# Two-bank PSUM tiles written whole before they are read, and other work moved between them, in a graph network layer

## The chip, the cores and the metric

The kernel runs on one core of a Trainium2 chip. The metric is device time in microseconds (us) of one execution. The engines of the core work side by side, each through its own list of instructions in order: TensorE (PE) multiplies matrices, VectorE (DVE) and ScalarE (ACT) work on elements, GpSimd (POOL) and SyncE (SP) here mostly start DMA transfers. An instruction waits until those whose results or buffers it needs are done. PSUM is the small memory that TensorE writes its results into; the kernel uses it in banks of 128 partitions by 512 fp32 numbers, two for each of its tiles.

## What is computed

One layer over 64 graphs of 256 nodes with 256 features (fp32). Cut to what matters:

```python
h = relu(layernorm(x))                                  # [64, 256, 256]
xc = h.transpose(0, 2, 1)
c = relu(bn1(conv1d(xc, conv1_w, pad=0)))               # 1 tap: 256 x 256 product
c = bn2(conv1d(c, conv2_w, pad=8))                      # 17 taps
x_conv = relu(c + xc).transpose(0, 2, 1)
s = h @ w_se.T + b_se                                   # 3 numbers for each node
dist = sq[:, :, None] + sq[:, None, :] - 2 * s @ s.T    # sq = sum(s * s)
A = exp(-dist) * adj
msg = relu(h @ w_msg.T + b_msg)
x_nmp = A @ msg
gi = concat(x_conv, x_nmp) @ w_ih.T + b_ih              # 3 gates of 256
gh = h @ w_hh.T + b_hh
r, z = sigmoid(gi_r + gh_r), sigmoid(gi_z + gh_z)
n = tanh(gi_n + r * gh_n)
out = x + (1 - z) * n + z * h
```

## The kernel before

The 64 graphs are worked on in pairs, numbered i = 0 to 31; a tile of one pair holds 2 x 256 = 512 nodes in its columns and 128 features in its partitions. Four pairs make a block, and there are eight blocks (b = 0 to 7; i = 4b is the block's first pair and nxt = i + 4 the next block's first). The trace's fifth block works on pairs 16 to 19.

**The convolution of 17 taps** is done for a block at once, by a transform along the nodes: conv1(j) (lines 673 to 688) makes each pair's input h, `split_steps` and `forward` (odd and even steps, which end with the tiles Sv, and U and PT) transform it on DVE (lines 59 to 65, with some scales on ACT, line 68), `begin(m)` and `complete(m)` (m = 0 to 7) multiply the bins by filters that SP streams from DRAM into nine buffers named wb, and the inverse (branch_back, odd_back, q_back, p_back, and a join for each pair) brings it back into Yv. `residual` (lines 817, 818) adds h and applies the relu for a pair. While a block's products run, the inputs of the block behind it are normalised (norm_steps), turned into feature-by-node layout by DMA (turn_h, sort_h, join_h; the result is hT) and run through conv1.

**Messages:** `message(i)` multiplies hT by w_msg and w_se on PE, adds the bias on DVE (line 830) and makes z, four small ACT operations, and the relu; `embed(i)` transposes z on PE and copies it into zT on ACT; `affinity(i)` multiplies zT with itself on PE, takes exp on ACT and multiplies by adj on DVE (line 868); `aggregate(i)` makes xnm from e and msg.

**Gates:** `gates(i)` (lines 1006 to 1074) forms the r and z gates as a block product with seven parts instead of eight, from hT, xnm and Yv (named "h", "xn", "xc") and sums of their quarters that DVE makes (sums_a line 937, sums_b line 945), in buffers wb that the filters give up for a while. `ghn(i)` (lines 995 to 1002) is the n gate's product of h, Gn that of the other inputs; DVE joins them (lines 1052, 1061), ACT takes tanh, DVE makes the output tr (lines 1069 to 1074), and `finish(i)` transposes it back, adds x and stores it (lines 1076 to 1091). Only the first pair of a block passes late_xc: its part 1 begins with h and xn, and the xc terms come once the inverse has got as far as this pair.

**What sets the order.** The order of each engine's list is that of the Python program, written by hand; gates takes functions (after5, fill, after7, after4, after) that it calls between its parts, and other work is put there. Only the DVE steps of the transforms float: they stand in a queue, `pace.vector` lets out as many as fit before the next DVE operation by a small model of PE's and DVE's time, and `pace.flush` lets out all up to a mark.

**PSUM.** All PE results go through two names, aux and acc, each with two buffers, and each buffer is a tile of two banks ([128, 2, 512] fp32). The third tile of a name waits until the readers of the first are done. All matmuls stand in the trace under the line of a helper, 516 (transposes 520), so a row is known by its output and inputs.

Of the kernel before, what the change touches and what calls it, by code (L numbers as in the profile page):

```python
# [300 lines left out]
def kernel(  # L301
# [372 lines left out]
    def conv1(i, bank=aux):  # L674
        if i >= B // G:
            return
        p = bank()
        for o in range(DC):
            for k in range(DC):
                mm(p[:, o], w_c1[:, k, o * P:(o + 1) * P], HT[i][:, k, :], W, start=(k == 0), stop=(k == DC - 1))  # L680
            v = h1.rearrange("p (g o) s b -> p o g s b", o=DC)[:, o, :, :, 1:1 + NW]
            u = p[:, o].rearrange("p (g s b) -> p g s b", g=G, b=NW)
            if i == 0:
                nc.vector.tensor_scalar(v, u, s1[:, o:o + 1], h1_shift[:, o:o + 1], ALU.mult, ALU.add)
                nc.vector.tensor_scalar(v, v, 0.0, None, ALU.max)
# [135 lines left out]
    def message(i):  # L821
        MSG[i] = work.tile([P, G, MC, D + SE], FP, name="msg")
        for g in range(G):
            p = aux()
            for c in range(MC):
                for k in range(DC):
                    mm(p[:, c, :D + SE], chunk(HT[i][:, k], g, c), w_msg[:, k, :], D + SE,
                       start=(k == 0), stop=(k == DC - 1))
            pace.vector(MC * D, pace.pe + PSUM)
            nc.vector.tensor_add(MSG[i][:, g], p[:, :, :D + SE], b_msg.unsqueeze(1).to_broadcast([P, MC, D + SE]))  # L830
        s = MSG[i][:, :, :, D:]
        flat = s.rearrange("p g c s -> p (g c) s")
# [61 lines left out]

    OT, SUM, ROLE = {}, {}, {}
    IN = ("h", "xn", "xc")
# [97 lines left out]

    def ghn(i):
        p = aux()
        gn = late.tile([P, DC, W], FP, name="gn")
        for dc in range(DC):
            for k in range(DC):
                n = 2 * D + dc * P  # L1000
                mm(p[:, dc], w_hh[:, k, n:n + P], HT[i][:, k, :], W, start=k == 0, stop=k == DC - 1)
            nc.scalar.activation(gn[:, dc], p[:, dc], AF.Identity, bias=b_hh[:, 2 * DC + dc:2 * DC + dc + 1])  # L1002
        return gn


    def gates(i, late_xc=None, after5=None, fill=None, after7=None, after4=None, after=None):
        A = acc()
        if late_xc:
            part(A[:, 0], 1, i, IN[:2], True)
            E5 = acc()  # L1010
            part(E5[:, 1], 5, i, IN[:2], True)
            gn = ghn(i)
            late_xc()
            part(A[:, 0], 1, i, IN[2:])
        else:
            part(A[:, 0], 1, i, IN, True)
            E5 = acc()
        nc.scalar.mul(E5[:, 0], A[:, 0], -1.0)  # L1018
        part(E5[:, 1], 5, i, IN[2:] if late_xc else IN, not late_xc)
        e = slot(ROLE["e"]).rearrange("p c d -> p (c d)")  # L1020
        nc.scalar.copy(e, E5[:, 1])
        if after5:
# [4 lines left out]
        nc.vector.tensor_add(A[:, 1], E5[:, 0], e)  # L1027
        if not late_xc:
            gn = ghn(i)
        if fill:  # L1030
# [127 lines left out]
    message(0)  # L1158
    filter_steps(7)
    embed(0)  # L1160
# [10 lines left out]
    for b in range(NB):  # L1171
# [6 lines left out]
        begin(1)  # L1178
        if b > 0:
            embed(i)  # L1180
        complete(0)
        complete(1)
        pace.add(fft.branch_back(Yv, T, 0))
        if b > 0:
            affinity(i)
            load_adj(i + 1)
            give("tz0", "tz1")
        begin(2)
        begin(3)
# [11 lines left out]
        pace.add(fft.branch_back(Yv, T, 2))  # L1201
        pace.add(fft.odd_back(Yv, T))
        aggregate(i)
        if b > 0:
# [4 lines left out]
        begin(4)  # L1209
        begin(5)  # L1210
        message(i + 1)
        complete(4)
        complete(5)
        embed(i + 1)
        pace.add(mix(fft.q_back(Yu, T), fft.odd_factors(Yv)))
        if b == 0:
            pace.add(norm_steps(nxt + 1)[0], normed[1])
            pace.add(weight_steps(), weighed)
        affinity(i + 1)
        if b > 0:  # L1220
            load_adj(i + 2)
            join_h(nxt)
        begin(6)
        begin(7)
        if b == 0:
            transpose_a(i + 1)
            transpose_h(nxt)
        complete(6)
        complete(7)
        pace.add(mix(fft.p_back(Yu, T), fft.q_factors(Yu)), scaled)  # L1230

# [20 lines left out]
        sums_a(i, "h")  # L1252
        sums_a(i, "xn")

# [13 lines left out]
        def after5():  # L1268
            if b == 0:
                transpose_a(i + 2)  # L1270
                load_y(0)
            else:
                load_adj(i + 3)
# [3 lines left out]

        def fill():
            join_h(nxt + 1)
            pace.flush(normed[2])  # L1280
            turn_h(nxt + 2)
# [4 lines left out]
        join(2)  # L1286
        gates(i, late_xc, after5, fill, None, None, after)
        pace.flush(halved)
# [10 lines left out]

        def fill():  # L1300
            join_h(nxt + 2)
# [18 lines left out]
        pace.flush(halved)  # L1320
        conv1(nxt + 3)
        pace.add(split_steps(nxt + 3), halved)
        if b + 1 < NB:
            forward()
        affinity(i + 3)

        def fill():
            pace.flush(normed[0])
            turn_h(nxt + 4)

        def after():
            pace.flush(joined[3])
            prepare(i + 3)
        gates(i + 2, None, lambda: finish(i + 1), fill, None, lambda: aggregate(i + 3), after)
        sort_h(nxt + 4)
# [3 lines left out]
        if b + 1 < NB:  # L1339
            pending.extend(TURNS)  # L1340

        def after7():
# [6 lines left out]
        gates(i + 3, None, lambda: finish(i + 2), lambda: join_adj(nxt), after7, after4)  # L1349
    finish(B // G - 1)  # L1350
# [45 lines left out]
```

## Time and profile before

| | |
|---|---|
| runs | 2216.42 and 2212.79 us, median 2214.61 |
| profiled execution | 2221.57 us, span 2219.6 us |
| mean granted TensorE clock | 0.929 of full speed |
| PE busy | 1902.7 us, 86% of the span |
| DVE busy | 1443.3 us, 65% |
| ACT busy | 852.3 us, 38% |

The profile and the trace are of that one profiled execution. In a row of the timeline the first number is the start in us, the second the time from the start of the first to the end of the last of the instructions put together in the row; then come engine, line, operation, output and inputs, shapes, how many, and in brackets how long the engine had stood idle before the row and which engine's operation let it go on. PE's clock is granted in two levels, shown as 0.50 and 1.00; a stretch with both shows a value between.

### The profile page before, as it was taken

How to read it: one execution, taken by the hardware profiler on the slowest of the kernel's cores; microseconds unless marked ns; L12 is line 12 of the kernel's file. 1: busy time of each engine (PE TensorE's matmuls, PEld its weight loads, DVE VectorE, ACT ScalarE, POOL GpSimd, SP SyncE). 2: the span in 40 equal slices, each digit the busy share in tenths (PEclk: the TensorE clock that was granted, in tenths of full speed). 3: DMA queues.
4: the chain of work that ended last, by engine and by line, in shares of the span. 5: the costliest groups of instructions: out<-in, count | busy, mean ns of one | idle time of the engine just before them, and what ended most of it. 6: DMA issues, size and time to landing. Idle time of an engine off the chain costs nothing. (4 is left out here: it accounts for less than half of the span.)

```text
span 2219.6 us, 24339 instructions
## 1 busy us (share of the span) xinstructions
PE 1902.7 (86%) x8614; PEld 1393.1 (63%) x8614; DVE 1443.3 (65%) x2599; ACT 852.3 (38%) x1600; POOL 219.0 (10%) x357
## 2 busy tenths in 40 slices
PE   5788889989899898898889888997988978998986
PEld 2467556766568565694567664685656845677654
DVE  3557647776488657875577764886477755777523
ACT  1434342363423533254423634236332544135321
POOL 2101011010011001010001100110010100101000
PEclk9979898999999899998989999999999989899988
DMA  6555333543247243364235432473333632153001
GB/s 169 178 182 179 95 76 77 177 122 88 67 119 223 68 88 84 102 198 97 74 77 170 126 90 67 118 212 84 89 83 112 188 91 71 40 182 107 20 19 29
DMA packets 250492, 246.11 MB, mean 111 GB/s; under 512 B 142936, under 2 KB 176500, under 8 KB 250371
## 3 DMA queue, kind: packets, MB, share of 16 engines
q1 hardware_dynamic: 216634, 183.83, 29.4%
q0 software_dynamic: 30784, 58.07, 10.2%
q10 hardware_dynamic: 2953, 2.66, 0.6%
q8 instruction: 68, 1.11, 0.2%
q14 instruction: 53, 0.43, 0.1%
HBM read 156.56 MB, written 44.30 MB: 90 GB/s over the span
## 5 line engine op out<-in xcount | busy, mean ns | idle before, releaser
L516 PE MATMUL acc<-wb,w_x 128*128 128x256 f32 x768 | 195.1, 405 | 58.4 <-DVE wb L937 29.0
L516 PEld LDWEIGHTS acc<-wb,w_x 128*128 128x128 f32 x768 | 149.4, 200 | 109.5 <-ACT acc L1018 36.2
L516 PE MATMUL acc<-xnm,w_ih 128*128 128x512 f32 (+1 forms) x512 | 206.8, 508 | 6.4 <-ACT wb L1044 6.4
L516 PE MATMUL acc<-Yv,w_ih 128*128 128x512 f32 (+1 forms) x512 | 201.1, 498 | 8.0 <-ACT Yv L818 8.0
L516 PE MATMUL aux<-hT,w_c 128*128 128x512 f32 x224 | 150.1, 806 | 59.1 <-ACT h L687 37.2
L1002 ACT ACTIVATE gn<-aux,bn_columns 128x512 f32<-128x512 f32 x64 | 44.0, 687 | 334.1 <-PE aux L516 334.1
L516 PEld LDWEIGHTS acc<-Yv,w_ih 128*128 128x128 f32 x512 | 101.9, 199 | 82.3 <-issue 64.1
L516 PE MATMUL aux<-hT,w_hh 128*128 128x512 f32 x256 | 128.4, 626 | 24.9 <-ACT gn L1002 24.9
L516 PEld LDWEIGHTS acc<-xnm,w_ih 128*128 128x128 f32 x512 | 103.1, 203 | 65.8 <-issue 45.9
L868 DVE TENSOR_TENSOR e<-e,adj 128x256 f32<-128x256 f32 x128 | 67.9, 593 | 109.3 <-ACT e L862 109.2
L516 PEld LDWEIGHTS aux<-hT,w_c 128*128 128x128 f32 x224 | 50.1, 242 | 138.3 <-ACT h L687 70.1
L516 PEld LDWEIGHTS acc<-U,wb 128*128 128x128 f32 x1024 | 131.0, 210 | 3.9 <-issue 2.0
L516 PE MATMUL acc<-U,wb 128*128 128x128 f32 x1024 | 132.6, 295 | 0.0
L516 PE MATMUL acc<-wb,w_ih 128*128 128x256 f32 x512 | 131.4, 379 | 0.0
L1064 ACT ACTIVATE gn<-gn,bn_columns 128x512 f32<-128x512 f32 x64 | 42.7, 714 | 224.5 <-DVE gn L1061 224.5
L516 PE MATMUL acc<-V,wb 128*128 128x128 f32 x1024 | 120.9, 280 | 8.3 <-ACT acc L778 8.3
L516 PEld LDWEIGHTS acc<-V,wb 128*128 128x128 f32 x1024 | 118.8, 196 | 9.7 <-ACT acc L778 9.7
L59 DVE SCALAR_TENSOR_TENSOR V<-T,V 128x256 f32<-128x256 f32 (+2 forms) x224 | 121.4, 606 | 0.3
L516 PE MATMUL aux<-w_msg,hT 128*128 128x259 f32 x512 | 117.5, 381 | 0.0
L1061 DVE SCALAR_TENSOR_TENSOR gn<-gn,acc 128x1024 f32<-128x1024 f32 x32 | 39.1, 1221 | 109.9 <-PE acc L516 109.9
L516 PEld LDWEIGHTS aux<-w_msg,hT 128*128 128x128 f32 x512 | 96.4, 189 | 21.1 <-issue 7.2
L1091 POOL DMA_DIRECT2D out_dram<-y x62 | 38.2, 621 | 722.6 <-DVE y L1086 686.4
(196 smaller groups left out, 3672.9 us busy)
## 6 DMA issues: line engine op xcount, KB each, us to landing
wb<-filt SPq DMA_DIRECT2D x376, 256.0 KB
y<-in_x_dram POOLq DMA_DIRECT2D x64, 256.0 KB, 4.3
out_dram<-y POOLq DMA_DIRECT2D x62, 256.0 KB, 5.1
x<-in_x_dram SPq DMA_DIRECT2D x60, 256.0 KB
halves_d<-halves SPq DMA_DIRECT2D x116, 128.0 KB
adjh<-halves_d POOLq DMA_DIRECT2D x116, 128.0 KB, 4.7
hh<-halves SPq DMA_DIRECT2D x108, 128.0 KB
filt<-fo POOLq DMA_DIRECT2D x18, 252.0 KB, 3.1
```

Of the source, the lines that this page charges most:

```text
L59: return self.step(out, lambda: self.v.scalar_tensor_tensor(out, x, s, y, op0=ALU.mult, op1=ALU.add))
L516: nc.tensor.matmul(p, w, v, **kw)
L868: nc.vector.tensor_mul(e, e, ADJ[i][:, g * MC + c].rearrange("p (b h c) -> p c h b", c=MC, b=NW))
L1002: nc.scalar.activation(gn[:, dc], p[:, dc], AF.Identity, bias=b_hh[:, 2 * DC + dc:2 * DC + dc + 1])
L1061: nc.vector.scalar_tensor_tensor(gn, gn, 0.5, Gn, op0=ALU.mult, op1=ALU.add)
L1064: nc.scalar.activation(gn[:, dc], gn[:, dc], AF.Tanh, bias=b_ih[:, 2 * DC + dc:2 * DC + dc + 1])
L1091: nc.gpsimd.dma_start(out=rows(out, G * i + g), in_=row_tile(Y[i], g))
```

## The change

Conv1 and ghn write both banks of their tile first, and ACT reads them after that. Part 5 of the gates gets a tile of its own (p5, an aux tile) where it used a bank of E5, into whose other bank ACT puts the negated part 1. Gn's tile is an aux tile and no longer an acc tile. In gates of a block's first pair, ghn is in two halves: the first in front of late_xc, the second behind part 6.

The ACT part of message becomes `message_out`, which may be called later. In the main loop embed and affinity stand later, behind another product or part; the sums of h and xn of the block's first pair stand ahead of the last inverse steps; finish moves from after5 to fill; the last pair's message stands ahead of conv1(nxt+2); conv1(nxt+3), forward and aggregate(i+3) move into gates(i+2), behind its part 4; turn_h moves behind part 7 or 4.

```diff
@@ conv1
             for k in range(DC):
                 mm(p[:, o], w_c1[:, k, o * P:(o + 1) * P], HT[i][:, k, :], W, start=(k == 0), stop=(k == DC - 1))
+        for o in range(DC):
             v = h1.rearrange("p (g o) s b -> p o g s b", o=DC)[:, o, :, :, 1:1 + NW]
@@ ghn
-    def ghn(i):
-        p = aux()
-        gn = late.tile([P, DC, W], FP, name="gn")
-        for dc in range(DC):
+    def ghn(i, dcs=range(DC)):
+        if 0 in dcs:
+            HN[i] = aux(), late.tile([P, DC, W], FP, name="gn")
+        p, gn = HN[i]
+        for dc in dcs:
             for k in range(DC):
                 n = 2 * D + dc * P
                 mm(p[:, dc], w_hh[:, k, n:n + P], HT[i][:, k, :], W, start=k == 0, stop=k == DC - 1)
+        for dc in dcs:
             nc.scalar.activation(gn[:, dc], p[:, dc], AF.Identity, ...)
@@ gates
             part(A[:, 0], 1, i, IN[:2], True)
-            E5 = acc()
-            part(E5[:, 1], 5, i, IN[:2], True)
-            gn = ghn(i)
+            p5 = aux()
+            part(p5[:, 0], 5, i, IN[:2], True)
+            ghn(i, (0,))
             late_xc()
...
         nc.scalar.mul(E5[:, 0], A[:, 0], -1.0)
-        part(E5[:, 1], 5, i, IN[2:] if late_xc else IN, not late_xc)
+        part(p5[:, 0], 5, i, IN[2:] if late_xc else IN, not late_xc)
...
-        if not late_xc:
-            gn = ghn(i)
+        gn = ghn(i, (1,) if late_xc else range(DC))
...
-        Gn = acc()
+        Gn = aux()
@@ main loop, each block
         complete(7)
+        sums_a(i, "h")
+        sums_a(i, "xn")
         pace.add(mix(fft.p_back(Yu, T), fft.q_factors(Yu)), scaled)
...
         message(i + 2)
-        embed(i + 2)
+        message_out(i + 2)
         conv1(nxt)
         pace.flush(normed[1])
         turn_h(nxt + 1)
-        affinity(i + 2)
+        embed(i + 2)
...
-        gates(i + 1, None, lambda: finish(i), fill, None, None, after)
+        gates(i + 1, None, None, fill, None, after4, after)
+        message(i + 3)
+        pace.flush(halved)
         conv1(nxt + 2)
+        message_out(i + 3)
...
-        message(i + 3)
-        join_h(nxt + 3)
-        embed(i + 3)
-        pace.flush(halved)
-        conv1(nxt + 3)
-        pace.add(split_steps(nxt + 3), halved)
-        if b + 1 < NB:
-            forward()
-        affinity(i + 3)
+        def after5():
+            embed(i + 3)
         def fill():
+            finish(i + 1)
+            affinity(i + 3)
+            join_h(nxt + 3)
+        def after4():
+            pace.flush(halved)
+            conv1(nxt + 3)
+            pace.add(split_steps(nxt + 3), halved)
+            if b + 1 < NB:
+                forward()
+            aggregate(i + 3)
             pace.flush(normed[0])
             turn_h(nxt + 4)
```

Three places of the order, before and now. First PE behind the gates of a block's second pair (the products of xnm and Yv with w_ih are Gn, w_c is conv1's weight, w_msg message's, z embed's). Before:

```order
L516 MATMUL acc<-xnm,w_ih 128x512 x2
L516 MATMUL acc<-Yv,w_ih 128x512 x2
L516 MATMUL aux<-hT,w_c_105 128x512 x4
L516 MATMUL aux<-w_msg,hT 128x259 x8
L520 MATMUL aux<-ident,z 128x128 x2
```

Now:

```order
L516 MATMUL aux<-xnm,w_ih 128x512 x2
L516 MATMUL aux<-Yv,w_ih 128x512 x2
L516 MATMUL aux<-w_msg,hT 128x259 x8
L516 MATMUL aux<-hT,w_c_105 128x512 x4
L516 MATMUL acc<-hT,w_hh 128x256
```

Message stands ahead of conv1(nxt+2), part 1 of the next gates follows conv1 at once, and Gn's, message's and conv1's tiles are now all of the name aux.

Second, DVE at the end of a block (tr is the output of the third pair, y that of the pair before it, msg is message's add, Sv the last odd step of the forward transform). Before:

```order
L1069 TENSOR_TENSOR tr<-hT,gn 128x1024
L1072 SCALAR_TENSOR_TENSOR tr<-wb_7610,tr 128x512
L1072 SCALAR_TENSOR_TENSOR tr<-wb_7619,tr 128x512
L1074 SCALAR_TENSOR_TENSOR tr<-tr,gn 128x1024
L1086 TENSOR_TENSOR y<-aux,y 128x1024
L62 TENSOR_TENSOR Sv<-V 128x2048
```

Now (here tr is that of the block's last pair):

```order
L59 SCALAR_TENSOR_TENSOR V<-T,V 128x16x16 x11
L1066 SCALAR_TENSOR_TENSOR gn<-gn,aux 128x1024
L1074 TENSOR_TENSOR tr<-hT,gn 128x1024
L1077 SCALAR_TENSOR_TENSOR tr<-wb_7783,tr 128x512
L1077 SCALAR_TENSOR_TENSOR tr<-wb_7792,tr 128x512
L1079 SCALAR_TENSOR_TENSOR tr<-tr,gn 128x1024
L831 TENSOR_TENSOR msg<-aux,b_msg 128x518 x2
L62 TENSOR_TENSOR Sv<-V 128x2048
```

The Sv step came in the middle of the last pair's gates, and now comes behind that pair's output and the next message's adds.

Third, ACT between conv1(nxt) and the first pair's ghn (h is conv1's result, Yv of line 818 or 819 the pair's relu, hh the start of the turn). Before:

```order
L838 ACTIVATE msg<-msg 128x2x256 x2
L846 COPY zT<-aux 128x128
L850 COPY zT<-aux 32x128 x8
L687 ACTIVATE h_160<-aux,bn_shift,bn_scale 128x2x16x16 x2
L68 ACTIVATE V<-V 128x16x2x16
L647 ACTIVATE hh<-x,shift,rstd 128x4x64 x4
L862 ACTIVATE e<-aux 128x512 x2
L818 ACTIVATE Yv<-Yv,bn_shift 128x512 x2
L1002 ACTIVATE gn<-aux,bn_columns 128x512 x2
```

Now:

```order
L841 ACTIVATE msg<-msg 128x2x256 x2
L688 ACTIVATE h_160<-aux,bn_shift,bn_scale 128x2x16x16 x2
L68 ACTIVATE Yv<-Yv 128x16x2x16 x4
L647 ACTIVATE hh<-x,shift,rstd 128x4x64 x4
L849 COPY zT<-aux 128x128
L853 COPY zT<-aux 32x128 x8
L1007 ACTIVATE gn<-aux,bn_columns 128x512
L68 ACTIVATE Yv<-Yv 128x16x2x16
L68 ACTIVATE V<-V 128x16x2x16 x3
L819 ACTIVATE Yv<-Yv,bn_shift 128x512 x2
```

The copies of zT come behind h, four scales and hh, and the first ghn half is read ahead of four more scales and the relu.

## Rows read from the trace of the kernel before

**Rows 1.** The page's first section: busy us, share of the span, instructions.

```profile
PE 1902.7 (86%) x8614; PEld 1393.1 (63%) x8614; DVE 1443.3 (65%) x2599; ACT 852.3 (38%) x1600; POOL 219.0 (10%) x357
```

**Rows 2.** Windows, blocks 1, 5, 8: us, busy (count) by engine, PEclk, DMA share, GB/s.

```profile
core 0: us, PE busy (x) PEld busy (x) DVE busy (x) ACT busy (x) POOL busy (x), PEclk, DMA share, GB/s
145.55:411.60 266.05, 233.39 (x1049) 172.17 (x1049) 177.37 (x329) 97.26 (x178) 25.25 (x39) 0.91 0.44 122
1189.80:1449.20 259.40, 227.36 (x1041) 167.10 (x1040) 177.96 (x319) 104.97 (x196) 25.47 (x40) 0.93 0.41 113
1968.00:2219.60 251.60, 209.09 (x1002) 161.13 (x1000) 124.50 (x203) 79.69 (x162) 14.34 (x24) 0.92 0.22 65
```

**Rows 3.** Half-clock windows: block 5's last, its five's sum, block 1's five's sum.

```profile
1420.27:1427.09 6.82, 6.05 (x19) 5.16 (x20) 4.13 (x3) 0.00 (x0) 1.21 (x2) 0.50 0.10 14
sum 34.12, PE 29.00 PEld 16.74 DVE 15.36 ACT 9.78 POOL 2.50; mean PE 5.80 PEld 3.35 DVE 3.07 ACT 1.96 POOL 0.50
...
sum 47.77, PE 42.85 PEld 27.02 DVE 26.59 ACT 15.75 POOL 4.40; mean PE 8.57 PEld 5.40 DVE 5.32 ACT 3.15 POOL 0.88
```

**Rows 4.** Timeline of PE in block 5: start, us, instructions, [idle before <- releaser].

```profile
1262.07 0.54 PE L520 MATMUL aux<-ident,z 128*128 128x128 f32 x2 [1.83 <-ACT z L834]
...
1278.19 3.78 PE L516 MATMUL acc<-wb,w_x 128*128 128x256 f32 x8 [4.61 <-DVE wb L937]
...
1285.40 1.98 PE L516 MATMUL aux<-hT,w_hh 128*128 128x512 f32 x4 [0.78 <-ACT gn L1002]
...
1314.35 1.98 PE L516 MATMUL aux<-hT,w_c 128*128 128x512 f32 x4 [1.63 <-ACT h L687]
...
1357.48 3.67 PE L516 MATMUL aux<-w_msg,hT 128*128 128x259 f32 x16
...
1366.76 3.78 PE L516 MATMUL aux<-hT,w_c 128*128 128x512 f32 x4 [3.13 <-ACT hT L670]
...
1401.33 3.62 PE L516 MATMUL aux<-e,msg 128*128 128x256 f32 x16
...
1415.14 2.86 PE L516 MATMUL acc<-wb,w_x 128*128 128x256 f32 x12 [0.73 <-ACT acc L1018]
...
1421.04 1.97 PE L520 MATMUL aux<-ident,tr 128*128 128x128 f32 x8 [3.04 <-DVE tr L1074]
...
1452.73 3.73 PE L516 MATMUL acc<-Sv,wb 128*128 128x128 f32 x32
```

**Rows 5.** Window from split to Sv's end, and DVE's timeline in block 5.

```profile
1376.15:1426.46 50.31, 45.09 (x179) 33.63 (x178) 42.72 (x66) 11.75 (x19) 6.02 (x10) 0.94 0.35 85
...
1275.44 2.10 DVE L868 TENSOR_TENSOR e<-e,adj 128x256 f32<-128x256 f32 x4
...
1361.40 1.29 DVE L830 TENSOR_TENSOR msg<-aux,b_msg 128x518 f32<-128x518 f32 x2
...
1411.86 1.22 DVE L1061 SCALAR_TENSOR_TENSOR gn<-gn,acc 128x1024 f32<-128x1024 f32 x1 [1.69 <-PE acc L516]
...
1419.76 1.22 DVE L1074 SCALAR_TENSOR_TENSOR tr<-tr,gn 128x1024 f32<-128x1024 f32 x1
```

**Rows 6.** Timeline of ACT in block 5.

```profile
1263.17 0.24 ACT L846 COPY zT<-aux 128x128 f32<-128x128 f32 x1
1263.32 2.12 ACT L850 COPY zT<-aux 32x128 f32<-32x128 f32 x8
...
1270.12 0.78 ACT L687 ACTIVATE h<-aux,bn_shift,bn_scale 128x512 f32<-128x512 f32 x1 [3.87 <-PE aux L516]
...
1271.32 2.06 ACT L647 ACTIVATE hh<-x,shift,rstd 128x256 f32<-128x256 f32 x4
```

**Rows 7.** Timelines of ACT, DVE and PE around the end of block 1's inverse.

```profile
235.20 1.65 ACT L68 ACTIVATE V<-V 128x512 f32<-128x512 f32 x3
...
236.89 0.69 DVE L62 TENSOR_TENSOR T<-V 128x512 f32<-128x512 f32 x1 [4.55 <-ACT V L68]
...
241.16 2.07 PE L516 MATMUL acc<-Yv,w_ih 128*128 128x256 f32 x4 [6.59 <-ACT Yv L818]
```

More of the change, by code (lines that the diff above doesn't have):

```diff
@@ L830, in message, with message_out @@
             nc.vector.tensor_add(MSG[i][:, g], p[:, :, :D + SE], b_msg.unsqueeze(1).to_broadcast([P, MC, D + SE]))
+    def message_out(i):
         s = MSG[i][:, :, :, D:]
@@ L891, in aggregate @@
         nc.scalar.activation(XNM[i], p, AF.Copy)
-    OT, SUM, ROLE = {}, {}, {}
+    OT, SUM, ROLE, HN = {}, {}, {}, {}
     IN = ("h", "xn", "xc")
@@ L1016, in gates @@
             part(A[:, 0], 1, i, IN, True)
-            E5 = acc()
+            p5 = aux()
+        E5 = acc()
         nc.scalar.mul(E5[:, 0], A[:, 0], -1.0)
-        part(E5[:, 1], 5, i, IN[2:] if late_xc else IN, not late_xc)
+        part(p5[:, 0], 5, i, IN[2:] if late_xc else IN, not late_xc)
         e = slot(ROLE["e"]).rearrange("p c d -> p (c d)")
-        nc.scalar.copy(e, E5[:, 1])
+        nc.scalar.copy(e, p5[:, 0])
         if after5:
@@ L1158 @@
     message(0)
-    filter_steps(7)
+    message_out(0)
+    filter_steps(8)
     embed(0)
@@ L1179 @@
         if b > 0:
+            message_out(i)
+        complete(0)
+        if b > 0:
             embed(i)
-        complete(0)
         complete(1)
         pace.add(fft.branch_back(Yv, T, 0))
+        begin(2)
         if b > 0:
@@ L1187 @@
             give("tz0", "tz1")
-        begin(2)
         begin(3)
@@ L1202 @@
         pace.add(fft.odd_back(Yv, T))
+        begin(4)
         aggregate(i)
+        begin(5)
         if b > 0:
@@ L1208 @@
             nc.gpsimd.dma_start(out=w_ih, in_=ih_wT.rearrange("(k p) o -> p k o", p=P))
-        begin(4)
-        begin(5)
+        complete(4)
         message(i + 1)
-        complete(4)
         complete(5)
-        embed(i + 1)
+        message_out(i + 1)
         pace.add(mix(fft.q_back(Yu, T), fft.odd_factors(Yv)))
@@ L1218 @@
             pace.add(weight_steps(), weighed)
+        begin(6)
+        begin(7)
+        embed(i + 1)
+        if b > 0:
+            join_h(nxt)
+        complete(6)
         affinity(i + 1)
@@ L1221 @@
             load_adj(i + 2)
-            join_h(nxt)
-        begin(6)
-        begin(7)
         if b == 0:
@@ L1227 @@
             transpose_h(nxt)
-        complete(6)
         complete(7)
+        sums_a(i, "h")
+        sums_a(i, "xn")
         pace.add(mix(fft.p_back(Yu, T), fft.q_factors(Yu)), scaled)
@@ L1248 @@
         turn_h(nxt + 1)
-        affinity(i + 2)
+        embed(i + 2)
         if b == 0:
             pace.flush(weighed)
-        sums_a(i, "h")
-        sums_a(i, "xn")
         def late_xc():
@@ L1269, in after5 @@
             if b == 0:
-                transpose_a(i + 2)
                 load_y(0)
@@ L1278, in fill, with after7 @@
         def fill():
+            affinity(i + 2)
+            if b == 0:
+                transpose_a(i + 2)
             join_h(nxt + 1)
+        def after7():
             pace.flush(normed[2])
@@ L1286 @@
         join(2)
-        gates(i, late_xc, after5, fill, None, None, after)
+        gates(i, late_xc, after5, fill, None, after7, after)
         pace.flush(halved)
@@ L1300, in fill @@
         def fill():
+            finish(i)
             join_h(nxt + 2)
+        def after4():
             join_adj(i + 3)
@@ L1316, with after4 @@
         keep_adj(nxt + 2)
-        message(i + 3)
-        join_h(nxt + 3)
-        embed(i + 3)
-        pace.flush(halved)
-        conv1(nxt + 3)
-        pace.add(split_steps(nxt + 3), halved)
-        if b + 1 < NB:
-            forward()
-        affinity(i + 3)
-        def fill():
+        def after5():
+            embed(i + 3)
+        def fill():
+            finish(i + 1)
+            affinity(i + 3)
+            join_h(nxt + 3)
+        def after4():
+            pace.flush(halved)
[4 more added lines that the diff above has]
+            aggregate(i + 3)
             pace.flush(normed[0])
@@ L1333, in after @@
             prepare(i + 3)
-        gates(i + 2, None, lambda: finish(i + 1), fill, None, lambda: aggregate(i + 3), after)
+        gates(i + 2, None, after5, fill, None, after4, after)
         sort_h(nxt + 4)
@@ L1340, with fill @@
             pending.extend(TURNS)
+        def fill():
+            finish(i + 2)
+            join_adj(nxt)
         def after7():
@@ L1348, in after4 @@
             load_kinds()
-        gates(i + 3, None, lambda: finish(i + 2), lambda: join_adj(nxt), after7, after4)
+        gates(i + 3, None, None, fill, after7, after4)
     finish(B // G - 1)
```

## The prediction

> **What bounds the kernel now.** I read the page's busy shares first [rows 1]: TensorE (PE) works 86% of the span, DVE 65%. PE is the bound, so only what PE loses can be won. Next I cut the trace into its eight blocks of eight graphs each and took one window for the fifth, the first and the last [rows 2]; the five others within look like the fifth. In the fifth block PE is busy 227.36 of 259.40 us, so it waits 32.0. Third, the granted clock: five stretches of that block ran at 0.50, the lower of the two levels (1.2 against 2.4 GHz), and each stretch begins during or just after one of the longer PE waits. PE was busy 29.00 us in them [rows 3]; the same matmuls at the higher level take half, so 14.5 us more are lost. A block thus loses 32.0 + 14.5 = **46.5 us** to waits and their aftermath. Everything below is about these 46.5 us, since the change adds no arithmetic and takes none away.
>
> The PE timeline of that block says where the 32 us lie [rows 4]. Each matmul leaves two records. The largest: 4.61 us before the first gate sums (released by a DVE sum), 3.13 and 3.04 us (ACT's copy of hT, DVE's tr), four waits of 1.63 us or less in front of conv1's second half on ACT's h, three of 1.2 to 1.9 us on z, four of 0.78 us in the middle of ghn, four of about 0.7 us in front of part 5. Long waits are followed by a stretch at half clock: the 3.04 us wait ends at 1421.04, and 1420.27 to 1427.09 runs at 0.50 [rows 3].
>
> **What goes.** Conv1 and ghn write one bank, ACT reads it, and PE stands still until that read is over, although its next matmul writes the other bank of the same tile: 1.63 and 0.78 us [rows 4], where the read itself takes 0.78 in conv1 [rows 6] and about as much in ghn. With both banks written first, these waits vanish and the reads fall behind PE's next work. Here the Trainium skill has a rule against the change: "Perfetto Trace Analysis", section "Matmuls", says that independent matmul groups should rotate through PSUM banks so that the evacuation of one overlaps the next group's matmuls, which is what alternating write and read was meant to give. The rows show no such overlap, since the waits are at least about as long as the reads, so the trace decides for the change; by the rule the waits would be worth nothing to remove and the reads would come later, which is the first rival below. The part-5 waits go too, as the product no longer writes the tile that ACT negates into. The z waits are covered by conv1 or products placed between, and the 4.61 us wait goes because the sums of h and xn now stand ahead of the inverse transform. So nearly all of the 46.5 us goes; the question is **which waits take its place**. I find six, from the order of the changed program with durations from rows. A long wait also costs time at half clock afterwards; before, 32.0 us of waits brought 14.5, or 0.45 us for each, and I take a little less, 0.41 for each us of a new one.
>
> 1. *begin(0) of the next block waits for Sv.* forward() now starts after conv1(nxt+3), which has moved behind part 4 of gates(i+2). From the aggregate there to begin(0) PE took 51.4 us (1401.33 to 1452.73 [rows 4]), of which 4.55 are waits that go or move and 3.0 half clock: 43.8 us of work. On DVE the old stretch from split to Sv held 42.72 us of work [rows 5]; out of it go the four e products (2.1) and one y (1.2, as other rows of 1024 columns), into it come two more gn steps (2.4), a tr group (3.7) and the message adds (1.3): 46.8. With 1.6 of waits for tanh, 0.5 of small ones, and a start 1.65 after conv1's end, Sv is ready at 50.6. PE waits 50.6 − 43.8 = 6.8, and 2.8 are lost at half clock after it: **9.6** (range 5 to 12).
> 2. *begin(4) waits for the last U step*, the next on the same DVE line: **0.9**.
> 3. *ghn's first half in gates(i)* takes the aux buffer that embed used, which comes free when ACT has copied zT. ACT's line from conv1's end is now: h twice (1.5), hh (2.06), zT (0.24 + 2.12) [rows 6], and four scales between (2.2, as three take 1.65 [rows 7]): 8.1. PE has some 4 us of parts 1 and 5 in front: wait 4.5, aftermath 1.8: **6.3** (3 to 8).
> 4. *Part 1's xc terms wait for the end of the inverse.* ACT's read of that ghn half stands ahead of four scales, then come DVE's four join steps, the residual and ACT's relu: 0.7 + 2.2 + 2.7 + 0.7 + 0.7 = 7.1. Block 1 of the old kernel has the same chain already, with three scales, and PE waited 6.59 in it [rows 7]. With 2.9 of aftermath: **10.0** (7 to 12). The old 4.61 us wait had this chain ahead of it as well, but other PE work hid most of it.
> 5. *conv1(nxt+2) waits for the message's first add.* Message now stands ahead of conv1, and its adds stand on DVE behind the last gn step, the six sums and the tr group. From that gn step to the end of tr took 9.1 us (1411.86 to 1420.98 [rows 5]), with an add of 0.7 behind it about 9.85 us from Gn's end. PE has message in between (3.67 [rows 4]): wait 6.4, aftermath 2.6: **9.0** (6 to 10).
> 6. *Small ones:* affinity's halves behind ghn's reads and y (1.1), part 5's own tile (0.5), z (0.6): **2.2** (1 to 5).
>
> What is moved beyond these costs nothing as far as I see: the hh turns and their transposing DMAs leave later, but their results are used a pair later, and SP's filter loads keep their order; finish in fill is two PE groups earlier than its buffer is wanted. If that cover were gone, one hh chain (2.06 on ACT, then DMA) would be next on PE's path.
>
> **The sum.** After the change a block loses 9.6 + 0.9 + 6.3 + 10.0 + 9.0 + 2.2 = 38.0 instead of 46.5: 8.5 us less, six times, 51. Block 1 had more to lose: 266.05 − 233.39 = 32.7 us of waits [rows 2] and half of 42.85 us at half clock, 21 [rows 3], together 54, of which items 3 to 5 and one more stay, 26: 28 us won. The last block has no next transform and no conv1 behind it; I take one inner block's gain there, 8. Together 87, against the profiled execution's 2221.57 (span 2219.6): 2135. That execution is 7.0 us (0.3%) above the median of the runs, 2214.61, so the median should be about **2128**. With all terms at their low ends a block loses 23 (gain 23.5, six times 141, in all 177: about 2038), which would need every guess wrong one way; with all at their high ends 48 (about 2190). Half of either distance gives this case's own range, 2083 to 2160.
>
> **Rivals.** *PSUM pressure* (0.17): there are still two aux buffers, and now Gn, the fifth product and both banks of conv1 and ghn go through them. A tile written whole is read later and handed on later. If each of eight places a block hands on its buffer one activation later (0.7 us) and PE is there waiting, 5.6 us a block or 45 us in all come back: about 2173, within 2%. For it: the 3.13 us waits show PE arriving before its operands; against it: ACT is busy only 104.97 of 259.40 us in the fifth block [rows 2], and most hand-outs have a gate part between. The Trainium skill's "Perfetto Trace Analysis", "Optimization Strategy", takes a gap that repeats on the busiest engine for a sign of too little PSUM for the next tile; if so, widening what each tile waits for makes the gaps longer, and that is this rival.
> *The inverse stays hidden* (0.08): if ACT reaches the scales before ghn's half, item 4 goes; 10.0 × 7 = 70 more: about 2058.
> *The DVE line becomes the bound* (0.08), slower than before: everything from conv1(nxt+3) to Sv and on to the last U step is one serial DVE line that PE waits for at begin(0). DVE has 42.72 of 50.31 us filled there already [rows 5]. Each us longer is a us per block. It decides from 8.6 us more than I reckoned, where the whole gain is gone; the old stretch held 7.6 us of DVE waits. If these and the gn steps' waits both stay in line (16 us), seven transitions lose 7.5 us net each: about 2267.
> *It does not do what it says* (0.03): if the scheduler put a read between conv1's halves, those waits, some 8 us a block [rows 4], would stay: 58 less gained over seven blocks, about 2186. The order shows the matmuls in one row.
>
> **Chances.** Forecast 0.64, pressure 0.17, inverse hidden 0.08, DVE line 0.08, not done 0.03. A change of 2% (44 us, to 2170 or 2259) is about what a measurement of this kernel can tell from none. Faster by over 2%: the forecast but a tenth of it for its upper tail, plus the hidden inverse and half the pressure: 0.70. Within: 0.21. Slower: 0.09, the DVE line and a little. The range of 8 in 10 leaves out the DVE line and the ends of the others: 2070 to 2205.
>
> **What would show it.** ghn and conv1 as one row of eight records without a wait in between (step right); PE's waits per block near 28 and half clock near 10 us instead of 32 and 14.5; the longest waits on Sv at begin(0), on Yv in gates(i), on the message add or h at conv1(nxt+2), on zT at ghn. If begin(0) does not wait at all, item 1 is wrong and the gain doubles; if it waits over 15 us, the third rival holds. If many waits of 0.7 us appear in front of aux tiles, the first does.

## The result and the profile after

The changed kernel takes 2082.05 us (median of 2078.63 and 2085.47) against 2214.61: a ratio of 0.9401, 95% interval 0.9327 to 0.9476. That is 132.6 us less, where 87 were forecast; 2128 was the predicted time, and the range of 2070 to 2205 holds the measured one; the narrower range that the prediction gives for the forecast itself, 2083 to 2160, misses it by 1 us. The profiled execution took 2078.63 us (span 2076.9), 3.4 below its median where that of before was 7.0 above, so between the two traces there are 142.7 us of span to account for.

The page's first section of the changed kernel, against [rows 1]:

```profile
PE 1814.5 (87%) x8614; PEld 1374.3 (66%) x8614; DVE 1442.2 (69%) x2599; ACT 848.1 (41%) x1600; POOL 218.5 (11%) x357
```

No work was taken away, yet PE's busy time fell by 88 us. So more than half of the gain does not show as idle time at all. The windows of the same three blocks, against [rows 2]:

```profile
135.81:383.46 247.65, 220.32 (x1056) 168.56 (x1055) 168.26 (x318) 97.25 (x179) 25.95 (x40) 0.94 0.47 131
1115.24:1359.48 244.24, 217.50 (x1041) 165.24 (x1041) 177.74 (x320) 104.58 (x196) 25.11 (x40) 0.93 0.44 120
1847.59:2076.90 229.31, 199.75 (x1000) 158.70 (x1000) 137.25 (x224) 79.09 (x162) 14.34 (x24) 0.93 0.25 72
```

Each row runs from one begin(0) to the next, the last one to the end. Those in [rows 2] are cut every 259.4 us from 411.60 on, up to 3.5 us ahead of begin(0). Cut at begin(0), block 1, blocks 2 to 7 and block 8 before are:

```profile
145.55:413.09 267.54, 234.88 (x1056) 173.45 (x1056) 178.86 (x333) 98.09 (x179) 25.25 (x39) 0.91 0.43 121
413.09:1968.12 1555.03, 1361.45 (x6241) 1002.37 (x6240) 1065.81 (x1905) 627.80 (x1172) 150.15 (x238) 0.94 0.41 111
1968.12:2219.60 251.48, 208.97 (x1001) 161.03 (x999) 124.39 (x202) 79.69 (x162) 14.34 (x24) 0.92 0.22 65
```

The fifth block keeps its 259.4 us (1193.32 to 1452.73). The equal cuts made all inner blocks look like it; from begin(0) to begin(0) the second takes 261.5 us and the sixth 254.0. The four stretches of the span, with the forecast beside them:

| stretch | before | after | gained | forecast |
|---|---|---|---|---|
| ahead of block 1 | 145.55 | 135.81 | 9.7 | 0 |
| block 1 | 267.54 | 247.65 | 19.9 | 28 |
| blocks 2 to 7 | 1555.03 | 1464.13 | 90.9 | 51 |
| block 8 | 251.48 | 229.31 | 22.2 | 8 |

In the fifth block PE now waits 244.24 − 217.50 = 26.7 us, where it waited 32.0. These are its waits (PE's timeline; the last row is the end of the block and belongs to the next):

```profile
1142.13 2.02 PE L516 MATMUL acc<-U,wb 128*128 128x128 f32 x16 [1.10 <-DVE U L62]
...
1171.36 3.95 PE L516 MATMUL aux<-e,msg 128*128 128x256 f32 x16 [0.43 <-DVE e L871]
...
1189.99 3.78 PE L516 MATMUL aux<-hT,w_hh 128*128 128x512 f32 x4 [4.07 <-ACT zT L853]
1200.88 2.07 PE L516 MATMUL acc<-Yv,w_ih 128*128 128x256 f32 x4 [7.11 <-ACT Yv L819]
...
1274.29 6.63 PE L516 MATMUL aux<-hT,w_c 128*128 128x512 f32 x8 [6.41 <-DVE msg L831]
...
1296.35 1.48 PE L863 MATMUL aux<-zT 9*128 9x256 f32 x8 [0.54 <-ACT gn L1007]
...
1359.48 6.72 PE L516 MATMUL acc<-Sv,wb 128*128 128x128 f32 x32 [6.71 <-issue]
```

The waits that stood in [rows 4] are gone: no row names h, z or ACT's negation any more, and seven others stand in their place (three more are under 0.15 us). "issue" in the last row means that the profile found no releaser; DVE's timeline names it:

```profile
1352.15 1.23 DVE L1074 TENSOR_TENSOR tr<-hT,gn 128x1024 f32<-128x1024 f32 x1 [1.46 <-ACT gn L1069]
...
1355.88 1.29 DVE L831 TENSOR_TENSOR msg<-aux,b_msg 128x518 f32<-128x518 f32 x2
1357.09 2.28 DVE L62 TENSOR_TENSOR Sv<-V 128x2048 f32<-128x2048 f32 x1
```

Sv ends at 1359.37, and begin(0) starts at 1359.48. At half clock PE was busy 4.58 + 8.05 + 5.95 = 18.6 us in the block's three stretches (against [rows 3]), which costs 9.3 instead of 14.5. The first stretch begins ahead of the block, while PE still waits for Sv:

```profile
1112.99:1119.82 6.83, 4.58 (x21) 4.62 (x22) 6.80 (x4) 0.57 (x1) 0.00 (x0) 0.50 0.14 41
1188.08:1205.15 17.07, 8.05 (x14) 4.64 (x15) 9.51 (x20) 6.92 (x16) 0.00 (x0) 0.50 0.56 130
1270.00:1280.24 10.24, 5.95 (x7) 2.53 (x8) 4.67 (x6) 0.00 (x0) 0.00 (x0) 0.50 0.64 102
```

So of the block's 15.2 us, 5.3 are waits and 5.2 are clock. The other 4.7 were in no term of the prediction. Two pieces of PE's timeline show most of them. First conv1 before, at full clock, with its wait in the middle:

```profile
1352.15 1.88 PE L516 MATMUL aux<-hT,w_c 128*128 128x512 f32 x4
1355.66 1.98 PE L516 MATMUL aux<-hT,w_c 128*128 128x512 f32 x4 [1.63 <-ACT h L687]
```

and the same eight records after:

```profile
1305.63 3.60 PE L516 MATMUL aux<-hT,w_c 128*128 128x512 f32 x8
1309.06 3.62 PE L516 MATMUL aux<-e,msg 128*128 128x256 f32 x16
```

From conv1's start to the next row, message's [rows 4], it is 1357.48 − 1352.15 = 5.33 us before and 1309.06 − 1305.63 = 3.43 after: 1.90 less, of which the row's bracket shows 1.63. A stall thus costs about 0.27 us more than its wait: the matmul ahead of it cannot overlap its end with the next (a step of 0.43 us within a row, as 3.60 − 1.88 for four records; 0.59 for the last one), and the first one behind it takes some 0.1 longer. The profile models where a matmul ends, so only the 1.90 is free of that model. The Trainium skill, "TensorE: Matmul & The Clock Gate", section "Step-by-step: what each phase is for", says that the drain of one matmul overlaps the fill of the next, and that a single isolated one cannot hide it; the rows agree, with 0.16 us for that part. PE's timeline of the block has 24 stalls before and 10 after, counting those over 60 ns: 14 × 0.27 = 3.8 of the 4.7. The remaining 0.9 us I cannot assign.

### The profile page after: what moved, and what is told of

Its sections match the earlier page's. It is cut to its first block, busy times and chain, and to the rows that moved or that the text cites. A ratio compares the mean times of both kernels' runs of the same rounds, so it can differ in the third digit from the quotient of the medians.

```text
span 2076.9 us, 24317 instructions
## 1 busy us (share of the span) xinstructions
PE 1814.5 (87%) x8614; PEld 1374.3 (66%) x8614; DVE 1442.2 (69%) x2599; ACT 848.1 (41%) x1600; POOL 218.5 (11%) x357
## 4 chain that ended last, share of the span: by engine, by line
PE 64%; DVE 20%; ACT 6%; issue 4%; ACTq 0%; DVEq 0%
PE acc L516 32%; PE aux L516 30%; DVE V L59 4%; DVE wb L948 2%; DVE T L59 1%; DVE gn L1066 1%; DVE wb L940 1%; DVE y L1091 1%; PE aux L520 1%; ACT zT L853 1%; DVE tr L1077 1%; DVE e L871 1%; ACT Yv L68 1%; DVE tr L1079 1%; DVE U L59 1%
## 5 line engine op out<-in xcount | busy, mean ns | idle before, releaser
L516 PE MATMUL aux<-hT,w_c 128*128 128x512 f32 x224 | 117.2, 672 | 44.9 <-DVE msg L831 44.9
L516 PE MATMUL acc<-Yv,w_ih 128*128 128x256 f32 x256 | 83.4, 417 | 56.8 <-ACT Yv L819 56.8
L65 DVE TENSOR_TENSOR V<-h 128x512 f32<-128x512 f32 x64 | 43.9, 686 | 121.3 <-ACT h L688 121.3
L516 PE MATMUL acc<-U,wb 128*128 128x128 f32 x1024 | 118.7, 275 | 7.8 <-DVE U L62 7.8
L516 PEld LDWEIGHTS acc<-U,wb 128*128 128x128 f32 x1024 | 117.4, 192 | 9.8 <-ACT Yv L790 8.9
L516 PE MATMUL acc<-Sv,wb 128*128 128x128 f32 x512 | 80.3, 327 | 46.9 <-issue 46.9
L516 PE MATMUL aux<-Yv,w_ih 128*128 128x512 f32 x256 | 120.3, 592 | 0.0
L516 PE MATMUL aux<-xnm,w_ih 128*128 128x512 f32 x256 | 120.3, 592 | 0.0
L516 PEld LDWEIGHTS acc<-Sv,wb 128*128 128x128 f32 x512 | 77.0, 241 | 52.3 <-issue 52.3
L516 PE MATMUL aux<-e,msg 128*128 128x256 f32 x464 | 106.9, 383 | 2.6 <-DVE e L871 2.6
```

The lines of the kernel that those rows point to most:

```text
L65: return self.step(out, lambda: self.v.tensor_sub(out, x, y))
L516: nc.tensor.matmul(p, w, v, **kw)
```

## The experiments

Each was compared with the kernel before on the same chip; the ratio's interval is 0.001 to 0.003 to each side. The changed kernel stands at 0.9401 of it, 2082 us.

**e1_whole.** The kernel before, with two lines added: conv1's and ghn's reads after both banks.

```diff
+        for o in range(DC):
             v = h1.rearrange(...)[:, o, :, :, 1:1 + NW]
...
+        for dc in range(DC):
             nc.scalar.activation(gn[:, dc], p[:, dc], AF.Identity, ...)
```

> The kernel before, with conv1 and ghn alone written whole and then read. Theory A (a stall of TensorE costs its visible wait and about 0.27 us more at its two ends, since the matmul ahead of it and the one behind it are not overlapped): eight waits of 0.78 to 1.63 us a block go, 8.3 us, and with their ends 2.2 us more, 10.5 a block over seven blocks, and some 6 us in the part ahead of block 1: about 2135. Theory B (the visible waits alone): about 2150. Theory C (PSUM pressure: reads come later and hold up the next tile): 2170 or more.

Measured: 2132.55 us, ratio 0.9622 (0.9592 to 0.9653). Theory A's number, but not by its working. The fifth block's window:

```profile
1145.66:1394.83 249.17, 221.47 (x1041) 166.55 (x1040) 177.88 (x321) 104.23 (x196) 25.24 (x40) 0.95 0.43 118
```

The sum of its five half-clock windows:

```profile
sum 23.89, PE 21.11 PEld 14.12 DVE 14.25 ACT 12.38 POOL 2.67; mean PE 4.22 PEld 2.82 DVE 2.85 ACT 2.48 POOL 0.53
```

Two rows of its PE timeline:

```profile
1310.59 0.54 PE L520 MATMUL aux<-ident,z 128*128 128x128 f32 x2 [3.80 <-ACT z L835]
...
1321.63 0.70 PE L861 MATMUL aux<-zT 9*128 9x256 f32 x4 [0.96 <-ACT h L688]
```

The block is 10.2 us shorter, but its waits only fell from 32.0 to 27.7: one wait on z grew from 1.94 to 3.80, and the reads of h, now later, hold up affinity's tile by 0.9. That is what theory C names, worth some 4 us a block. The clock made up for it: half-clock busy time fell from 29.0 to 21.1, worth 4.0. The remaining 1.9 us fit the ends of the eight stalls that went (24 to 16), 0.24 each. PSUM pressure is there, and far too small to turn the sign.

**e2_fifth.** The kernel before, with the fifth product alone in an aux tile.

```diff
-            E5 = acc()
-            part(E5[:, 1], 5, i, IN[:2], True)
+            p5 = aux()
+            part(p5[:, 0], 5, i, IN[:2], True)
...
+        E5 = acc()
         nc.scalar.mul(E5[:, 0], A[:, 0], -1.0)
```

> The kernel before, with the fifth product alone in an aux tile of its own. Four waits of about 0.7 us a block on ACT's negation go. Theory A: with their ends 3.9 us a block, about 2184. Theory B: 2.8 a block, about 2192. Theory C (an aux buffer more in use delays ghn and embed): 2215 or more.

Measured: 2187.56, ratio 0.9871 (0.9842 to 0.9901). Alone, this part brings 1.3%, which refutes C: in the fifth block the four waits are gone, and those on ghn and z are as long as before (the one on tr grew, from 3.04 to 4.14). A and B, 8 us apart, cannot be told from each other, as the interval is over 6 us to each side.

**e3_interleaved.** The changed kernel with the reads of conv1 and ghn put back between the banks (e1's lines taken out).

> The changed kernel with conv1 and ghn written and read bank by bank again. Theory A: seven waits come back a block, some 8 us, and 1.9 of their ends; seven blocks and the part ahead of block 1: about 2155. Theory B: about 2140. Theory C (the reads come earlier and give their tiles back earlier): 2110 or less.

Measured: 2153.35, ratio 0.9715 (0.9687 to 0.9743): 71 us slower than the changed kernel, as A has it. This is the clean case for the ends of the stalls, since the clock does not change (half-clock busy 18.5 us against 18.6). The fifth block's window, and the sum of its half-clock windows (the last of them lies at the next block's start, where the block's own first holds the same 4.2 us):

```profile
1162.62:1415.21 252.59, 219.00 (x1041) 164.39 (x1041) 178.12 (x320) 105.30 (x196) 25.25 (x40) 0.95 0.43 116
sum 27.30, PE 18.50 PEld 11.08 DVE 14.35 ACT 3.70 POOL 0.00; mean PE 4.62 PEld 2.77 DVE 3.59 ACT 0.93 POOL 0.00
```

The waits are 33.6 us, 6.9 more than in the changed kernel, and PE is busy 1.5 us longer with the same work at the same clock. Seven waits on h and gn are back, one on y comes in, and three of the changed kernel's small ones go, so there are 15 stalls instead of 10 by the count above: 0.3 us for each of five (0.2 for each of seven, when those under 0.15 us are left out).

**e12_moves.** The changed kernel with e3's edit, the fifth product back in E5 and Gn back in acc, so that only the moved work differs from before.

```diff
-            p5 = aux()
-            part(p5[:, 0], 5, i, IN[:2], True)
+            E5 = acc()
+            part(E5[:, 1], 5, i, IN[:2], True)
...
-        Gn = aux()
+        Gn = acc()
```

> The changed kernel with conv1 and ghn read bank by bank, the fifth product back in E5's tile and Gn back in acc: what is moved alone is left. If the parts add up (the whole tiles 71 to 85, the fifth product 27 to 30, of 133), 2153 + 28 = 2181, so the moves alone bring about 33 against the kernel before. Rival (the moves only work with the new tiles, since four new waits of 4 to 7 us come with them): 2215 or more.

Measured: 2160.78, ratio 0.9762 (0.9746 to 0.9779): the moves alone bring 52, more than the 33 expected. The parts do not add up: alone, the whole tiles bring 82, the fifth product's tile 27 and the moves 52, 161 together, and the change 133. The fifth product's tile and Gn's bring only 7 on top of the moves (2160.8 to 2153.4; 10 by the ratios). Four rows of PE in gates(i) and around it say why:

```profile
1238.39 1.98 PE L516 MATMUL aux<-hT,w_c 128*128 128x512 f32 x4 [1.77 <-ACT h L687]
...
1243.88 1.88 PE L516 MATMUL aux<-hT,w_hh 128*128 128x512 f32 x4
1254.48 2.08 PE L516 MATMUL acc<-Yv,w_ih 128*128 128x256 f32 x4 [8.72 <-ACT Yv L818]
1257.23 2.08 PE L516 MATMUL acc<-wb,w_x 128*128 128x256 f32 x4 [0.67 <-ACT acc L1021]
```

The four 0.7 us waits are back (one is shown), but ghn (hT and w_hh) no longer waits for zT, which cost the changed kernel 4.07 and e3 3.42: with the fifth product out of aux, ghn's tile is one that was free. Yv's wait takes back 1.6 of that.

The next four each take away one of the new waits.

**e4_scales.** The last scales of the inverse ahead of ACT's read of ghn.

```diff
+            pace.flush(scaled)
             ghn(i, (0,))
```

> The changed kernel with the transform's last scales ahead of ACT's read of ghn's first half. Theory A (that read holds up the chain to Yv): the 7.11 us wait falls to about 2.7, with half of the clock's aftermath less: 5.8 a block, about 2038. Rival (the chain is bound by DVE's own steps or by the copies of zT): the wait stays above 6, and the time within 10 us of the changed kernel's 2082.

Measured: 2050.10, ratio 0.9245 (0.9214 to 0.9277): 32 us less than the changed kernel. ACT's timeline, the changed kernel first:

```profile
1193.81 0.69 ACT L1007 ACTIVATE gn<-aux,bn_columns 128x512 f32<-128x512 f32 x1 [3.87 <-PE aux L516]
1194.39 0.62 ACT L68 ACTIVATE Yv<-Yv 128x512 f32<-128x512 f32 x1
1194.91 1.65 ACT L68 ACTIVATE V<-V 128x512 f32<-128x512 f32 x3
```

and with the edit:

```profile
1181.13 0.63 ACT L68 ACTIVATE Yv<-Yv 128x512 f32<-128x512 f32 x1
1181.67 1.65 ACT L68 ACTIVATE V<-V 128x512 f32<-128x512 f32 x3
1184.98 0.69 ACT L1007 ACTIVATE gn<-aux,bn_columns 128x512 f32<-128x512 f32 x1 [1.66 <-PE aux L516]
```

PE's timeline with the edit:

```profile
1187.63 2.08 PE L516 MATMUL acc<-Yv,w_ih 128*128 128x256 f32 x4 [2.69 <-ACT Yv L819]
```

ACT stood idle for 3.87 us in front of a read whose matmuls were still running, with work behind it that could have gone on. The wait fell to 2.69 (2.7 expected); a block gained 5.3 us instead of 5.8, and the time is 12 us above the 2038 expected.

**e5_sv and e9_conv.** Two ways to take away the wait on Sv. e5 puts Sv ahead of the last output on DVE; e9 moves conv1(nxt+3) and the forward transform from behind part 4 to the end of fill.

```diff
@@ e5_sv
-        gates(i + 3, None, None, fill, after7, after4)
+        gates(i + 3, None, None, fill, after7, after4, lambda: pace.flush(odd))
@@ e9_conv
         def after5():
             embed(i + 3)
+            join_h(nxt + 3)
         def fill():
             finish(i + 1)
             affinity(i + 3)
-            join_h(nxt + 3)
-        def after4():
             pace.flush(halved)
             conv1(nxt + 3)
             pace.add(split_steps(nxt + 3), halved)
             if b + 1 < NB:
                 forward()
+        def after4():
             aggregate(i + 3)
```

> The changed kernel with the Sv step ahead of the last pair's output tr and the next message's adds on DVE. Theory A (these 5 us stand between and are the cause of the 6.71 us wait at begin(0)): the wait falls below 0.5, with the clock's aftermath 9 a block, about 2020. Theory B (the cause is that the whole DVE line from conv1(nxt+3) to the last U step starts late): begin(0) waits for nothing, but PE then waits 8 to 9.5 us instead of 1.10 for the U step at begin(4), and the time falls by 2 a block at most: about 2070.

> The changed kernel with conv1(nxt+3) and the forward transform at the end of fill in gates(i+2), 8 us earlier on PE, with join_h in after5. Theory B (the DVE line from conv1(nxt+3) to U starts late): begin(0)'s 6.71 and begin(4)'s 1.10 us go, with the aftermath 8 to 11 a block: about 2015. Theory A (tr and the adds in front of Sv are the cause): the wait at begin(0) stays above 4, since tr cannot come earlier, and the time falls by 20 at most: about 2065.

Measured: e5 2067.49, ratio 0.9336 (0.9318 to 0.9353); e9 2001.84, ratio 0.9043 (0.9027 to 0.9059). Theory B holds in both. In e5 begin(0)'s wait is 0.23 us, and begin(4)'s grew from 1.10 to 5.16. Two rows of e5's DVE timeline:

```profile
1126.79 2.12 DVE L871 TENSOR_TENSOR e<-e,adj 128x256 f32<-128x256 f32 x4
...
1135.71 1.22 DVE L62 TENSOR_TENSOR U<-U 128x1024 f32<-128x1024 f32 x1
```

and begin(4) in PE's:

```profile
1137.19 3.47 PE L516 MATMUL acc<-U,wb 128*128 128x128 f32 x16 [5.16 <-DMA wb<-filt]
```

The bracket names a filter's DMA, but the U step ends at 1136.93 and PE starts 0.26 later, exactly as in the changed kernel (1386.85 and 1387.11), where the bracket names U. The lag is 0.26 in all seven blocks of e5, also in the two whose brackets name U. The wait is shorter than B's 8 us because DVE's line itself got shorter by an idle stretch: in the changed kernel the e products in it waited 3.69 us for ACT, and in e5 they do not. The two rows in the changed kernel:

```profile
1376.68 2.16 DVE L871 TENSOR_TENSOR e<-e,adj 128x256 f32<-128x256 f32 x4 [3.69 <-ACT e L865]
...
1385.63 1.22 DVE L62 TENSOR_TENSOR U<-U 128x1024 f32<-128x1024 f32 x1
```

In e9 both waits are gone, and Yv's as well, from 7.11 to 1.39, which neither theory had and whose cause stays open; a new one on the e products comes in (0.43 to 3.28). All of e9's waits over 0.6 us in a block:

```profile
1129.26 5.56 PE L516 MATMUL aux<-e,msg 128*128 128x256 f32 x16 [3.28 <-DVE e L871]
1148.47 3.78 PE L516 MATMUL aux<-hT,w_hh 128*128 128x512 f32 x4 [3.04 <-ACT zT L853]
1153.63 2.07 PE L516 MATMUL acc<-Yv,w_ih 128*128 128x256 f32 x4 [1.39 <-ACT Yv L819]
...
1227.06 6.63 PE L516 MATMUL aux<-hT,w_c 128*128 128x512 f32 x8 [6.42 <-DVE msg L831]
```

**e6_msg.** The last pair's message behind conv1(nxt+2) again.

```diff
-        message(i + 3)
         pace.flush(halved)
         conv1(nxt + 2)
+        message(i + 3)
         message_out(i + 3)
```

> The changed kernel with the last pair's message behind conv1(nxt+2) again, as it stood before the change. Theory A (the 6.41 us wait is that of conv1's aux tile for the message's first add, which stands behind sums and tr on DVE): the wait goes, and with its ends and the clock's aftermath 9 a block over seven blocks: about 2019. Rival (DVE is late anyway, so the wait moves to the fifth product's tile or to embed): a wait of 4 us or more there, and the time within 15 us of the changed kernel's 2082.

Measured: 2023.28, ratio 0.9146 (0.9132 to 0.9159): 59 us less than the changed kernel, theory A. The wait of 6.41 leaves 0.24 behind in front of the fifth product:

```profile
1234.41 1.88 PE L516 MATMUL aux<-hT,w_c 128*128 128x512 f32 x4
1236.13 3.73 PE L516 MATMUL aux<-w_msg,hT 128*128 128x259 f32 x16
...
1242.69 2.86 PE L516 MATMUL aux<-wb,w_x 128*128 128x256 f32 x12 [0.24 <-DVE msg L831]
```

DVE's adds come no earlier (9.05 us behind the last gn step in both kernels); PE has conv1 and part 1 to do until they are through.

**e7_hh.** embed's copies of zT ahead of the turn's hh.

```diff
+        embed(i + 2)
         pace.flush(normed[1])
         turn_h(nxt + 1)
-        embed(i + 2)
```

> The changed kernel with embed's copies of zT ahead of the turn's hh on ACT. Theory A (the 4.07 us wait of ghn's first half is ACT's line of h, scales, hh and zT): it falls by hh's 2.07 to 2.0, Yv's wait stays at 7.11 since all behind moves with it, and with a part of the aftermath 2 to 3 a block: about 2064. Rival (the zT copies wait for the transposes or for z): no change, 2082.

Measured: 2073.03, ratio 0.9375 (0.9359 to 0.9391): 9 us less than the changed kernel by the medians, half of what was expected. Its rows behave as theory A says: 2.20 instead of 4.07 in front of ghn, 7.10 in front of Yv. Against 0.9401 with its wider interval the gain in time is not certain.

**e10_all and e11_all.** The edits of e4, e6, e7 and e9 together; e11 adds e5's.

> The changed kernel with four edits together: the scales ahead of ghn's read, zT ahead of hh, message behind conv1(nxt+2), conv1(nxt+3) in fill. If the four waits are independent, the gains add up but for that of hh, which only shortens a wait that ends with the scales: 32 + 59 + 80 and 3 more, 1908 from 2082, with waits of about 5 us left a block. Rival (DVE, 178 us busy a block, now has no slack and holds PE at begin(0) or in front of the U step): 1940 or more, with such a wait of over 4 us.

> The kernel of e10_all, and the Sv step ahead of the last pair's output tr as in e5_sv. If Sv is no longer waited for once conv1(nxt+3) stands in fill, no change (within 6 us of e10_all). If a wait at begin(0) is left, it goes, and the time falls by that wait times seven, with no wait at begin(4) in its place.

Measured: e10 1904.01, ratio 0.8612 (0.8582 to 0.8642); e11 1908.00, ratio 0.8626 (0.8594 to 0.8658). The gains add up (178 us, against 32 + 59 + 80 + 9 = 180 one by one), and Sv's place no longer matters. e10 is 310 us below the kernel before and 178 below the changed one. Its page's first section:

```profile
PE 1770.8 (93%) x8614; PEld 1343.5 (71%) x8614; DVE 1439.3 (76%) x2599; ACT 850.4 (45%) x1600; POOL 218.1 (11%) x357
```

A block's window:

```profile
1024.63:1243.08 218.45, 210.24 (x1041) 161.04 (x1040) 177.36 (x320) 104.89 (x196) 25.10 (x40) 0.99 0.51 134
```

PE's waits over 1 us in that block:

```profile
1080.47 5.32 PE L516 MATMUL aux<-e,msg 128*128 128x256 f32 x16 [3.33 <-DVE e L871]
...
1097.57 1.98 PE L516 MATMUL aux<-hT,w_hh 128*128 128x512 f32 x4 [1.16 <-ACT zT L853]
1100.99 1.13 PE L516 MATMUL acc<-Yv,w_ih 128*128 128x256 f32 x4 [1.44 <-ACT Yv L819]
```

PE waits 8.2 us of 218.45, and the granted clock is 0.99, from 0.93.

## Why the prediction was right, and where its sizes were off

**The waits were right one by one.** Forecast and measured in the fifth block: begin(0) on Sv 6.8 and 6.71; begin(4) on U 0.9 and 1.10; ghn on zT 4.5 and 4.07; Yv 7.1 and 7.11; conv1 on the message 6.4 and 6.41; the small ones 2.2 and 1.3, with three under 0.15. The clock's aftermath 10.1 and 9.3. Item 1 holds term by term too: from the aggregate to Sv's end (1309.06 to 1359.37) DVE worked 46.3 us, with 46.8 reckoned, and PE 43.6, with 43.8. e4, e6, e7 and e9 show that each wait has the cause that was named: taking it away took the wait away, or the part expected (Yv's fell to 2.69, ghn's to 2.20). For Sv the cause was put down as one line of work from conv1's end; e5 and e9 show that it is that line's late start. The output and adds in front of Sv only decide whether Sv or U is waited for.

Some sums of the prediction do not come out as printed: 8.1 less 4 is 4.1 in item 3, item 4's terms make 7.0, and 9.85 less 3.67 is 6.2 in item 5. That Yv's and the message's waits were met to 0.01 us is in part luck. The shares named for "faster" add up to 0.74, not to 0.70.

**The gain per block was mis-sized: 8.5 forecast, 15.2 measured.** The forecast counted as lost before only idle time and half clock, 46.5 us. By the same count the changed block loses 26.7 + 9.3 = 36.0, where 38.0 were forecast: 1.2 less of waits and 0.8 less at half clock. The other 4.7 us lie in PE's busy time. The ends of stalls, which the prediction put at nothing, are 3.8 of them for the 14 stalls that went, at 0.27 each (e1 and e3 give 0.24 and 0.30); 0.9 stay open.

**The clock's price was right only in sum.** The prediction took 0.41 us at half clock for each us of a new wait. A block of the changed kernel waits 26.7 us and loses 9.3 to the clock, which is 0.35; but one of e12 waits 34.5 and loses 7.6, one of e9 waits 15.1 and loses 8.7, and one of e10 waits 8.2 and loses 1.6. So waits do not have one price.

**Block 1 was over-estimated** (28, measured 19.9): its list of what stays left out item 1, whose wait of 6.71 stands at this block's end as well. With its 9.6, the 28 become 18.4, and the ends of seven stalls that went (22 to 15) are 1.9 more. That the sum comes so close is in part luck: ghn's wait on zT is 2.08 in this block instead of 4.5, and a wait of 2.73 on e was not in the list.

**The stretch ahead of block 1 was forgotten** (0, measured 9.7): conv1 is called four times there as well, and its waits on h (2.95, 0.93, 0.87 and 0.87) went. Others grew, so idle time fell by 3.1 us only (145.55 − 97.39 to 135.81 − 90.75); the rest is busy time, with a granted clock of 0.95 instead of 0.91. That part is not steady: e4, e5, e6, e7 and e9 leave this stretch as it is in the changed kernel, and it takes 141.1, 139.7, 136.6, 138.1 and 136.5 us in them.

**Block 8 was under-estimated** (8, measured 22.2): "one inner block's gain" was taken, not this block's own rows. Before the change the last block had the longest z wait of all, since no conv1 stood between message and embed:

```profile
2123.92 0.69 PE L520 MATMUL aux<-ident,z 128*128 128x128 f32 x2 [7.28 <-ACT z L834]
```

The change puts embed behind part 5 there, and this wait goes. The block's idle time fell by 13.0 us in all (251.48 − 208.97 to 229.31 − 199.75), although Yv's wait grew from 1.39 to 7.62 and one of 3.73 on the message's add came in.

**The rivals.** PSUM pressure exists (e1: z and affinity wait longer), but took back only half of the idle time that e1 saved, and the clock and the ends of stalls outweigh it. The Trainium skill's rule in "Perfetto Trace Analysis", section "Matmuls", is that independent matmul groups rotate through PSUM banks. As the prediction applied it to the two banks of a tile, e1 should have gained nothing; it gained 3.8%. In the kernel before, the matmuls into the second bank of conv1's tile waited 1.63 us for the read of the first [rows 4], so alternating between the two was no rotation. Items 3 and 5 are waits for an aux tile too, forecast one by one; the many waits of 0.7 us in front of aux tiles that were this rival's sign did not come in the changed kernel. The hidden inverse and the late DVE line did not come; DVE's line does bound begin(0), at the price forecast.

## What to carry to other kernels

A wait in the middle of a matmul group costs more than its idle time: about 0.27 us of busy time at its two ends here, and often a stretch at half clock behind it, so count stalls as well as their sum. When a change removes many short waits and brings a few long ones, work out each new one from the queue in front of its releaser; then most of them can be taken away by moving one call. Cost every stretch of the program by its own rows, the first and the last blocks too: three of the mis-sized terms here came from not doing so.

## What the runs showed of the hardware

- A stall of PE cost 0.27 us more than the idle time that the profile shows for it (conv1, 128x512 fp32, full clock: 1.90 us between the same rows, with a wait of 1.63). Over a block, e1 and e3 give 0.24 and 0.30 a stall.
- Half clock went with the waits, not with the work: with 8.2 us of waits a block instead of 32.0, the granted clock of the same matmuls was 0.99 instead of 0.93. It was not in proportion to them: e12 lost 7.6 us to it with 34.5 us of waits, e9 lost 8.7 with 15.1.
- A bracket can name a DMA where a DVE step ends the wait: in all seven blocks of e5 PE started 0.26 us after the U step, the same lag as where U was named.
